# Scores computed transposed, softmax without the row maximum, row sums from a ones column beside V

## Chip, cores and metric

The kernel runs on one core of a Trainium2 chip. The metric is the device time of one execution in microseconds (us), from three executions; lower is better. TensorE (PE in the profile) does matrix products, VectorE (DVE), ScalarE (ACT) and GpSimd (POOL) do elementwise work, SyncE (SP) issues most transfers. PEld is TensorE's loading of weights, which the profile shows apart from the products.

## The reference

Input x has 128 graphs of 128 nodes with 768 features, adj is one 128x128 matrix a graph, about one entry in eight above zero. All is float32.

```python
h = jnp.maximum(_layernorm(x, axis=-1), 0.0)
q = _split_heads(h @ Wq + bq)            # 12 heads of 64
k = _split_heads(h @ Wk + bk)
v = _split_heads(h @ Wv + bv)
scores = jnp.einsum('bhqd,bhkd->bhqk', q, k) / jnp.sqrt(64)
scores = scores + beta * adj_e           # beta = 0.1
scores = jnp.where(adj_e > 0, scores, -9e15)
probs = jax.nn.softmax(scores, axis=-1)
out = jnp.einsum('bhqk,bhkd->bhqd', probs, v)
return x + out.transpose(0, 2, 1, 3).reshape(128, 128, 768)
```

## The kernel before

The 128 graphs go through in 32 groups G of four graphs g. Nodes lie on the 128 partitions. In a group the twelve heads go in six pairs; a pair is called oc, the same index as the 128 columns of Wq and Wk that belong to it, and j (0 or 1) is the head in the pair. So there are 32 x 6 = 192 pairs.

For each group, `norm` (lines 95 to 108) makes the normalised rows xn on VectorE with a power on GpSimd, and `to_hT` (110 to 116) transposes them on TensorE (tile pt) and takes them out of PSUM on ScalarE with the relu. `project_v` (118 to 127) makes V of the group with 96 matmul instructions of 384 columns. Every float32 matmul in the code is two matmul instructions in the trace; a transpose is one.

For each pair, `project_qk` (129 to 142) makes transposed Q and K of the four graphs, 12 instructions of 512 columns each (tiles pwq and pwk); VectorE takes Q out of PSUM, ScalarE takes K out. `scores` (144 to 165) makes 8 score blocks of 128x128 (tile sc; two heads on the upper and the lower 64 rows of the array). A row of a block is a query. Then, for each head of the pair and all four graphs at once, GpSimd fills a tile t with -9e15 (line 156), VectorE adds beta x adj (157), copies where adj is above zero (158) and reduces to the negative row maximum (160). ScalarE takes the exponential in 8 instructions a pair, one for each graph and head since the maximum is its bias, each with the row sum as a by-product that is read out by an instruction of its own (162). `transpose_probs` (167 to 176) transposes the 8 blocks on TensorE (tile ppt) and copies them out on ScalarE (pT), since the product with V needs keys on the partitions. `attend` (178 to 191) multiplies with V (tile av, 16 instructions of 64 columns), divides by the row sums on VectorE (187) and adds to x on GpSimd (189). When a group's last pair is added, SyncE sends its x out, and the x tile's next load waits for that.

The main loop (200 to 222) is a software pipeline over pairs: projections of pair i, transposes of pair i-1's probabilities, scores of pair i, product with V of pair i-1. Layer norm of the next group is placed in pairs 0 to 3 and its transposes in pairs 4 and 5. PSUM tiles of the tag mm (projections and pt) have three buffers, sc, pt two each, av one.

The order of instructions on each engine is not that of the code. A scheduler of the framework lays them out when the program is built, by its own estimates of times and by which buffers come free; each engine then runs its list strictly in that order and waits where an operand or a buffer is missing.

Of the kernel before, what the change touches and what calls it, by code (L numbers as in the profile page):

```python
# [9 lines left out]
F32 = mybir.dt.float32  # L10
U8 = mybir.dt.uint8
# [8 lines left out]
MASKED = -9000000000000000.0  # L20


@with_exitstack
def kernel(
# [26 lines left out]
    VH = D // 2  # L51
    SCALE = 1.0 / math.sqrt(HD)
# [8 lines left out]
    xs, bias, keep, xn, hT, vs = {}, {}, {}, {}, {}, {}  # L61
# [5 lines left out]
    def load_adj(G):  # L67
        a = big.tile([P, GRP, N], F32, tag="adj", name=f"adj_{G}")
        nc.sync.dma_start(a, adj[G * GRP:(G + 1) * GRP].rearrange("g q k -> q g k"))
        bias[G] = big.tile([P, GRP, N], F32, tag="bias", name=f"bias_{G}")  # L70
        nc.vector.tensor_scalar(bias[G], a, beta_c, None, op0=ALU.mult)
# [3 lines left out]
    load_x(0)  # L75
    ident = const.tile([P, P], F32, name="ident")
    make_identity(nc, ident)
    nhalf = const.tile([P, 1], F32, name="nhalf")
    nc.gpsimd.memset(nhalf, -0.5)
    beta_c = const.tile([P, 1], F32, name="beta_c")  # L80
# [29 lines left out]
    def to_hT(G, c):  # L110
        if c == 0:
            hT[G] = big.tile([P, NC, W], F32, tag="hT", name=f"hT_{G}")
        p = psum.tile([P, W], F32, tag="mm", name=f"pt_{G}_{c}", bufs=3)
        for g in range(GRP):
            nc.tensor.transpose(p[:, g * N:(g + 1) * N], xn[G][:, g, c * P:(c + 1) * P], ident)  # L115
        nc.scalar.activation(hT[G][:, c, :], p, AF.Relu)  # L116

    def project_v(G):
        vs[G] = big.tile([P, GRP, D], F32, tag="v", name=f"v_{G}")
        for g in range(GRP):  # L120
            for s in range(2):
                p = psum.tile([P, VH], F32, tag="mm", name=f"pv_{G}_{g}_{s}", bufs=3)
                for c in range(NC):
                    nc.tensor.matmul(p, hT[G][:, c, g * N:(g + 1) * N],  # L124
                                     w_sb["wv"][:, c, s * VH:(s + 1) * VH],
                                     start=(c == 0), stop=(c == NC - 1))
                nc.vector.tensor_add(vs[G][:, g, s * VH:(s + 1) * VH], p, bv_b[:, s * VH:(s + 1) * VH])  # L127

    def project_qk(G, oc):
        got = []  # L130
        for name in ("wq", "wk"):
            p = psum.tile([P, W], F32, tag="mm", name=f"p{name}_{G}_{oc}", bufs=3)
            for c in range(NC):
                nc.tensor.matmul(p, w_sb[name][:, c, oc * P:(oc + 1) * P], hT[G][:, c, :],  # L134
                                 start=(c == 0), stop=(c == NC - 1))
            t = work.tile([P, W], F32, tag=name, name=f"{name}T_{G}_{oc}", bufs=2)
            if name == "wq":
                nc.vector.tensor_scalar(t, p, bq_c[:, oc:oc + 1], SCALE, op0=ALU.add, op1=ALU.mult)  # L138
            else:
                nc.scalar.activation(t, p, AF.Identity, bias=bk_c[:, oc:oc + 1])  # L140
            got.append(t)
        return got

    def scores(G, oc, qT, kT):
        ps = [psum.tile([P, GRP, N], F32, tag="sc", name=f"sc_{G}_{oc}_{j}") for j in range(2)]
        for g in range(GRP):
            for j in range(2):
                r = slice(j * HD, (j + 1) * HD)
                nc.tensor.matmul(ps[j][:, g, :], qT[r, g * N:(g + 1) * N], kT[r, g * N:(g + 1) * N],  # L149
                                 start=True, stop=True)  # L150
        pr = []
        rs = stat.tile([P, 2, GRP], F32, tag="rs", name=f"rs_{G}_{oc}")
        sm = stat.tile([P, 2, GRP], F32, tag="sm", name=f"sm_{G}_{oc}")
        for j in range(2):
            t = work.tile([P, GRP, N], F32, tag="t", name=f"t_{G}_{oc}_{j}")
            nc.gpsimd.memset(t, MASKED)  # L156
            nc.vector.tensor_add(ps[j], ps[j], bias[G])  # L157
            nc.vector.copy_predicated(t, keep[G], ps[j])  # L158
            nmax = stat.tile([P, GRP], F32, tag="nmax", name=f"nmax_{G}_{oc}_{j}")
            nc.vector.tensor_reduce(nmax, t, AX.X, ALU.max, negate=True)  # L160
            for g in range(GRP):
                nc.scalar.activation(t[:, g, :], t[:, g, :], AF.Exp, bias=nmax[:, g:g + 1],  # L162
                                     accum_out=sm[:, j, g:g + 1])
            pr.append(t)
        return pr, sm, rs

    def transpose_probs(G, oc, pr):
        pT = []
        for j in range(2):
            p = psum.tile([P, GRP, N], F32, tag="pt", name=f"ppt_{G}_{oc}_{j}")  # L170
            for g in range(GRP):
                nc.tensor.transpose(p[:, g, :], pr[j][:, g, :], ident)  # L172
            t = work.tile([P, GRP, N], F32, tag="pT", name=f"pT_{G}_{oc}_{j}")
            nc.scalar.copy(t, p)  # L174
            pT.append(t)
        return pT

    def attend(G, oc, pT, sm, rs):
        nc.vector.reciprocal(rs, sm)
        pa = psum.tile([P, GRP, 2, HD], F32, tag="av", name=f"av_{G}_{oc}", bufs=1)  # L180
        for j in range(2):
            for g in range(GRP):
                h = 2 * oc + j
                nc.tensor.matmul(pa[:, g, j, :], pT[j][:, g, :], vs[G][:, g, h * HD:(h + 1) * HD],  # L184
                                 start=True, stop=True)
        o = work.tile([P, GRP, 2, HD], F32, tag="o", name=f"o_{G}_{oc}", bufs=2)
        nc.vector.tensor_mul(o, pa, rs.rearrange("p j g -> p g j")[:, :, :, None].to_broadcast([P, GRP, 2, HD]))  # L187
        xo = xs[G][:, :, oc * P:(oc + 1) * P]
        nc.gpsimd.tensor_add(xo, xo, o.rearrange("p g j d -> p g (j d)"))  # L189
# [3 lines left out]
    load_adj(0)  # L193
# [58 lines left out]
```

## Time and profile before

| what | value |
|---|---|
| median of three executions | 3869.4 us (3868.63 to 3870.0) |
| profiled execution: span from first to last instruction | 3866.2 us (its time beside the span is not given) |
| TensorE matmul busy, share of the span | 3825.9 us, 99% |
| TensorE weight loads busy | 2239.4 us, 58% |
| VectorE / ScalarE / GpSimd busy | 1402.0 / 1026.0 / 513.2 us (36%, 27%, 13%) |
| chain that ended last | PE 99%, DMA 1% |
| mean granted TensorE clock | 0.998 |

The chain of waits is followed back from the last instruction: at each step to what released it, or to the instruction before it on its engine. Its pieces add up to the span, so it tells what the time is made of, while busy times of one engine can overlap. A group row gives the busy time of all instructions of one line and shape, the mean duration of one, and the idle time before them with what ended it. Matmuls and weight loads are pipelined, so the mean duration of one is longer than its share of the busy time.

### The profile page before, as it was taken

Reading aid. Unit: us, or ns where it says so; the run is one execution under the profiler, and the core shown is the slowest. Engines: PE = TensorE matmul, PEld = TensorE weight load, DVE = VectorE, ACT = ScalarE, POOL = GpSimd, SP = SyncE. Lnnn points to the kernel's source line nnn. Section 1 sums busy time; section 2 is a strip of 40 time slices with the busy share of each in tenths; the row PEclk is TensorE's granted clock in tenths of the full one; section 3 lists DMA queues with packets and bytes.
Section 4 is the critical chain, followed back from the end, with each engine's and each line's share of the span. In section 5 each row is a group of like instructions: output and inputs, shape, how many; then the busy total and the mean of one; then the engine's idle time right before and its main releaser. Section 6 shows DMA issues by size and latency. Waiting matters only on the chain.

```text
span 3866.2 us, 41384 instructions
## 1 busy us (share of the span) xinstructions
PE 3825.9 (99%) x16128; PEld 2239.4 (58%) x16128; DVE 1402.0 (36%) x2688; ACT 1026.0 (27%) x3841; POOL 513.2 (13%) x711
## 2 busy tenths in 40 slices
PE   6999999999999999999999999999999999999998
PEld 3555555555555555555555555555555555555655
DVE  3343333333333433334333343333333333433323
ACT  1232222322222322223222232222332222322223
POOL 1011111111111111111111111111111111111111
PEclk9999999999999999999999999999999999999999
DMA  3000100100000100000010000000000000000000
GB/s 138 3 36 33 36 36 3 36 33 36 36 14 26 36 33 36 30 10 36 33 36 36 3 36 33 36 36 3 36 33 36 36 19 20 36 33 33 17 1 33
DMA packets 55330, 119.17 MB, mean 31 GB/s; under 512 B 3552, under 2 KB 19936, under 8 KB 55136
## 3 DMA queue, kind: packets, MB, share of 16 engines
q1 hardware_dynamic: 50688, 109.06, 7.7%
q10 hardware_dynamic: 4448, 7.48, 0.5%
q8 instruction: 127, 2.08, 0.2%
q14 instruction: 67, 0.55, 0.0%
HBM read 66.20 MB, written 50.33 MB: 30 GB/s over the span
## 4 chain that ended last, share of the span: by engine, by line
PE 99%; DMA 1%; issue 0%; DVE 0%; ACT 0%; POOL 0%; POOLq 0%
PE pwq L134 26%; PE pv L124 26%; PE pwk L134 26%; PE av L184 9%; PE sc L149 6%; PE ppt L172 4%; PE pt L115 2%; DMA x<-in_x_dram 0%; DMA adj<-in_adj_dram 0%; POOLq L247 0%; POOL x L189 0%; ACT L116 0%; DVE nmax L160 0%; DVE t L158 0%; DVE sc L157 0%
## 5 line engine op out<-in xcount | busy, mean ns | idle before, releaser
L134 PE MATMUL pwq<-hT,wq 128*128 128x512 f32 x2304 | 1032.5, 598 | 0.0
L134 PE MATMUL pwk<-hT,wk 128*128 128x512 f32 x2304 | 1020.1, 592 | 0.0
L124 PE MATMUL pv<-wv,hT 128*128 128x384 f32 x3072 | 996.0, 486 | 0.0
L124 PEld LDWEIGHTS pv<-wv,hT 128*128 128x128 f32 x3072 | 583.7, 190 | 413.9 <-issue 15.1
L134 PEld LDWEIGHTS pwk<-hT,wk 128*128 128x128 f32 x2304 | 437.8, 190 | 551.0 <-issue 543.4
L162 ACT ACTIVATE t<-t,nmax 128x128 f32<-128x128 f32 x1536 | 593.8, 392 | 486.4 <-DVE nmax L160 486.4
L134 PEld LDWEIGHTS pwq<-hT,wq 128*128 128x128 f32 x2304 | 422.9, 190 | 462.6 <-issue 452.5
L157 DVE TENSOR_TENSOR sc<-sc,bias 128x512 f32<-128x512 f32 x384 | 249.1, 694 | 979.6 <-PE sc L149 979.6
L127 DVE TENSOR_TENSOR v<-pv,bv_b 128x384 f32<-128x384 f32 x256 | 142.6, 557 | 1006.7 <-PE pv L124 1006.7
L156 POOL MEMSET t<- 128x512 f32 x384 | 189.2, 524 | 2262.9 <-PE ppt L172 2262.7
L174 ACT COPY pT<-ppt 128x512 f32<-128x512 f32 x384 | 204.5, 587 | 951.9 <-PE ppt L172 951.8
L140 ACT ACTIVATE wkT<-pwk,bk_c 128x512 f32<-128x512 f32 x192 | 131.9, 687 | 1193.0 <-PE pwk L134 1193.0
L184 PE MATMUL av<-v,pT 128*128 128x64 f32 x3072 | 385.4, 279 | 0.0
L189 POOL TENSOR_TENSOR x<-x,o 128x512 f32<-128x512 f32 x192 | 254.2, 1324 | 950.1 <-DVE o L187 950.1
L184 PEld LDWEIGHTS av<-v,pT 128*128 128x128 f32 x3072 | 359.0, 192 | 23.4 <-ACT pT L174 0.3
L162 ACT ACTIVATION_READ_ACCUMULATOR t<-t,nmax 128x1 f32 x1536 | 293.8, 191 | 0.0
L138 DVE TENSOR_SCALAR wqT<-pwq,bq_c 128x512 f32<-128x512 f32 x192 | 144.1, 751 | 355.9 <-PE pwq L134 353.5
L158 DVE COPY_PREDICATED t<-keep,sc 128x512 f32<-128x512 uint8 x384 | 255.7, 718 | 0.0
L160 DVE TENSOR_REDUCE nmax<-t 128x4 f32<-128x512 f32 x384 | 241.8, 670 | 0.0
L172 PEld LDWEIGHTS ppt<-ident,t 128*128 128x128 f32 x1536 | 180.2, 141 | 97.7 <-issue 90.0
L149 PE MATMUL sc<-wkT,wqT 64*128 64x128 f32 x3072 | 223.1, 285 | 0.0
L149 PEld LDWEIGHTS sc<-wkT,wqT 64*128 64x128 f32 x3072 | 186.3, 187 | 38.1 <-ACT wkT L140 32.3
(21 smaller groups left out, 1035.5 us busy)
## 6 DMA issues: line engine op xcount, KB each, us to landing
x<-in_x_dram SPq DMA_DIRECT2D x32, 1536.0 KB, 6.3
out_dram<-x SPq DMA_DIRECT2D x32, 1536.0 KB, 5.2
adj<-in_adj_dram SPq DMA_DIRECT2D x32, 256.0 KB, 2.5
wq<-in_L_gnn_Wq_dram ACTq DMA_DIRECT2D x6, 384.0 KB, 7.3
wk<-in_L_gnn_Wk_dram ACTq DMA_DIRECT2D x6, 384.0 KB, 9.1
wv<-in_L_gnn_Wv_dram ACTq DMA_DIRECT2D x6, 384.0 KB, 5.9
bv_b<-in_L_gnn_bv_dram ACTq DMA_DIRECT2D x1, 384.0 KB, 8.7
beta_c<-in_L_gnn_beta_dram ACTq DMA_DIRECT2D x1, 0.5 KB, 3.8
```

What stands on the lines that cost most here:

```text
L124: nc.tensor.matmul(p, hT[G][:, c, g * N:(g + 1) * N], w_sb["wv"][:, c, s * VH:(s + 1) * VH], start=(c == 0), stop=(c == NC - 1))
L134: nc.tensor.matmul(p, w_sb[name][:, c, oc * P:(oc + 1) * P], hT[G][:, c, :], start=(c == 0), stop=(c == NC - 1))
L149: nc.tensor.matmul(ps[j][:, g, :], qT[r, g * N:(g + 1) * N], kT[r, g * N:(g + 1) * N], start=True, stop=True)
L156: nc.gpsimd.memset(t, MASKED)
L157: nc.vector.tensor_add(ps[j], ps[j], bias[G])
L158: nc.vector.copy_predicated(t, keep[G], ps[j])
L160: nc.vector.tensor_reduce(nmax, t, AX.X, ALU.max, negate=True)
L162: nc.scalar.activation(t[:, g, :], t[:, g, :], AF.Exp, bias=nmax[:, g:g + 1], accum_out=sm[:, j, g:g + 1])
L172: nc.tensor.transpose(p[:, g, :], pr[j][:, g, :], ident)
L174: nc.scalar.copy(t, p)
L184: nc.tensor.matmul(pa[:, g, j, :], pT[j][:, g, :], vs[G][:, g, h * HD:(h + 1) * HD], start=True, stop=True)
L189: nc.gpsimd.tensor_add(xo, xo, o.rearrange("p g j d -> p g (j d)"))
```

## The change

The score product swaps its operands, so that a block comes out with keys on the partitions. The exponential of it can then go into the product with V as it is, and the transposes of the probabilities and their copies fall away. The row maximum, which would now lie across partitions, is not taken: VectorE does one instruction for each head (cap the score at 60, add the transposed bias), ScalarE one exponential of 128x512. Each head's V gets a 65th column of ones, which is filled once, so the product's 65th column is the row sum; it is raised to at least 1e-30, inverted and multiplied on VectorE. The product's tile av takes two PSUM banks, and mm gets four buffers in place of three.

The bias tile is new: `make_bias` makes beta x adj with -9e15 where adj is not above zero, transposes it on TensorE once a group (tile pb, four instructions), and ScalarE copies it out (biasT). It is called once ahead of the loop and then in pair 4 of each group but the last, for the next group.

Running maxima of the sums, of their inverses and of the squared bias are kept (`seen`, `seen_b`). After the last pair they are compared with caps (1e15, 1e15, 400), the result goes to a register of every engine, and a second program, `general`, runs behind a branch if a cap was passed. `general` is the same computation with the row maximum, one graph at a time, and writes all outputs anew.

The diff, cut to its core:

```diff
+SCORE_CAP = 60.0
+BIAS_CAP = 20.0
+SUM_CAP = 1e15
+TINY = 1e-30
...
+    bad = keep.tile([1, 1], I32, name="bad")
+    args = (x, adj, wq, bq, wk, bk, wv, bv, beta, out)
+    direct(tc, *args, bad)
+    again = nc.values_load(bad[0:1, 0:1])
+    with tc.If(again > 0):
+        general(tc, *args)
...
+    VE = HD + 1
...
-        a = big.tile([P, GRP, N], F32, tag="adj", name=f"adj_{G}")
-        nc.sync.dma_start(a, adj[G * GRP:(G + 1) * GRP].rearrange("g q k -> q g k"))
-        bias[G] = big.tile([P, GRP, N], F32, tag="bias", name=f"bias_{G}")
-        nc.vector.tensor_scalar(bias[G], a, beta_c, None, op0=ALU.mult)
-        keep[G] = big.tile([P, GRP, N], U8, tag="keep", name=f"keep_{G}")
-        nc.vector.tensor_scalar(keep[G], a, 0.0, None, op0=ALU.is_gt)
+        adjs[G] = big.tile([P, GRP, N], F32, tag="adj", name=f"adj_{G}", bufs=1)
+        nc.sync.dma_start(adjs[G], adj[G * GRP:(G + 1) * GRP].rearrange("g q k -> q g k"))
...
+    vs = [const.tile([P, GRP, HEADS, VE], F32, name=f"v{i}") for i in range(2)]
+    for v in vs:
+        nc.gpsimd.memset(v[:, :, :, HD:VE], 1.0)
...
-        p = psum.tile([P, W], F32, tag="mm", name=f"pt_{G}_{c}", bufs=3)
+        p = psum.tile([P, W], F32, tag="mm", name=f"pt_{G}_{c}", bufs=4)
...
+    def make_bias(G):
+        a = adjs[G]
+        b = work.tile([P, GRP, N], F32, tag="b", name=f"b_{G}", bufs=1)
+        nc.vector.tensor_scalar(b, a, beta_c, BIAS_CAP, op0=ALU.mult, op1=ALU.min)
+        kp = work.tile([P, GRP, N], U8, tag="kp", name=f"kp_{G}", bufs=1)
+        nc.vector.tensor_scalar(kp, a, 0.0, None, op0=ALU.is_gt)
+        bm = stat.tile([P, GRP], F32, tag="bm", name=f"bm_{G}", bufs=1)
+        b2 = work.tile([P, GRP, N], F32, tag="b2", name=f"b2_{G}", bufs=1)
+        nc.gpsimd.tensor_tensor(b2, b, b, ALU.mult)
+        nc.vector.tensor_reduce(bm, b2, AX.X, ALU.max)
+        nc.vector.tensor_tensor(seen_b, seen_b, bm, ALU.max)
+        nb = work.tile([P, GRP, N], F32, tag="nb", name=f"nb_{G}", bufs=1)
+        nc.gpsimd.memset(nb, MASKED)
+        nc.vector.copy_predicated(nb, kp, b)
+        p = psum.tile([P, GRP, N], F32, tag="mm", name=f"pb_{G}", bufs=4)
+        for g in range(GRP):
+            nc.tensor.transpose(p[:, g, :], nb[:, g, :], ident)
+        biasT[G] = big.tile([P, GRP, N], F32, tag="biasT", name=f"biasT_{G}")
+        nc.scalar.copy(biasT[G], p)
...
-                nc.vector.tensor_add(vs[G][:, g, s * VH:(s + 1) * VH], p, bv_b[:, s * VH:(s + 1) * VH])
+                nc.vector.tensor_add(v[:, g, s * HH:(s + 1) * HH, 0:HD],
+                                     p.rearrange("p (h d) -> p h d", d=HD),
+                                     bv_b[:, s * VH:(s + 1) * VH].rearrange("p (h d) -> p h d", d=HD))
...
-                nc.tensor.matmul(ps[j][:, g, :], qT[r, g * N:(g + 1) * N], kT[r, g * N:(g + 1) * N],
+                nc.tensor.matmul(ps[j][:, g, :], kT[r, g * N:(g + 1) * N], qT[r, g * N:(g + 1) * N],
                                  start=True, stop=True)
-        pr = []
-        rs = stat.tile([P, 2, GRP], F32, tag="rs", name=f"rs_{G}_{oc}")
-        sm = stat.tile([P, 2, GRP], F32, tag="sm", name=f"sm_{G}_{oc}")
+        es = []
         for j in range(2):
-            t = work.tile([P, GRP, N], F32, tag="t", name=f"t_{G}_{oc}_{j}")
-            nc.gpsimd.memset(t, MASKED)
-            nc.vector.tensor_add(ps[j], ps[j], bias[G])
-            nc.vector.copy_predicated(t, keep[G], ps[j])
-            nmax = stat.tile([P, GRP], F32, tag="nmax", name=f"nmax_{G}_{oc}_{j}")
-            nc.vector.tensor_reduce(nmax, t, AX.X, ALU.max, negate=True)
-            for g in range(GRP):
-                nc.scalar.activation(t[:, g, :], t[:, g, :], AF.Exp, bias=nmax[:, g:g + 1],
-                                     accum_out=sm[:, j, g:g + 1])
-            pr.append(t)
-        return pr, sm, rs
-
-    def transpose_probs(G, oc, pr):
-        pT = []
-        for j in range(2):
-            p = psum.tile([P, GRP, N], F32, tag="pt", name=f"ppt_{G}_{oc}_{j}")
-            for g in range(GRP):
-                nc.tensor.transpose(p[:, g, :], pr[j][:, g, :], ident)
-            t = work.tile([P, GRP, N], F32, tag="pT", name=f"pT_{G}_{oc}_{j}")
-            nc.scalar.copy(t, p)
-            pT.append(t)
-        return pT
-
-    def attend(G, oc, pT, sm, rs):
+            e = work.tile([P, GRP, N], F32, tag="e", name=f"e_{G}_{oc}_{j}")
+            nc.vector.scalar_tensor_tensor(e, ps[j], SCORE_CAP, biasT[G], op0=ALU.min, op1=ALU.add)
+            nc.scalar.activation(e, e, AF.Exp)
+            es.append(e)
+        return es
+
+    def attend(G, oc, es):
+        pa = psum.tile([P, 2, 512], F32, tag="av", name=f"av_{G}_{oc}", bufs=1)
+        for g in range(GRP):
+            for j in range(2):
+                at = ((g % 2) * 2 + j) * VE
+                nc.tensor.matmul(pa[:, g // 2, at:at + VE], es[j][:, g, :], vs[G % 2][:, g, 2 * oc + j, :],
+                                 start=True, stop=True)
+        got = pa[:, :, 0:4 * VE].rearrange("p a (b e) -> p a b e", e=VE)
+        sm = stat.tile([P, 2, 4, 1], F32, tag="sm", name=f"sm_{G}_{oc}")
+        nc.vector.tensor_scalar(sm, got[:, :, :, HD:VE], TINY, None, op0=ALU.max)
+        rs = stat.tile([P, 2, 4, 1], F32, tag="rs", name=f"rs_{G}_{oc}")
         nc.vector.reciprocal(rs, sm)
-        pa = psum.tile([P, GRP, 2, HD], F32, tag="av", name=f"av_{G}_{oc}", bufs=1)
-        for j in range(2):
-            for g in range(GRP):
-                h = 2 * oc + j
-                nc.tensor.matmul(pa[:, g, j, :], pT[j][:, g, :], vs[G][:, g, h * HD:(h + 1) * HD],
-                                 start=True, stop=True)
-        o = work.tile([P, GRP, 2, HD], F32, tag="o", name=f"o_{G}_{oc}", bufs=2)
-        nc.vector.tensor_mul(o, pa, rs.rearrange("p j g -> p g j")[:, :, :, None].to_broadcast([P, GRP, 2, HD]))
+        o = work.tile([P, 2, 4, HD], F32, tag="o", name=f"o_{G}_{oc}", bufs=2)
+        nc.vector.tensor_mul(o, got[:, :, :, 0:HD], rs.to_broadcast([P, 2, 4, HD]))
+        for i, t in enumerate((sm, rs)):
+            nc.vector.tensor_tensor(seen[:, i, :], seen[:, i, :], t.rearrange("p a b e -> p (a b e)"), ALU.max)
         xo = xs[G][:, :, oc * P:(oc + 1) * P]
-        nc.gpsimd.tensor_add(xo, xo, o.rearrange("p g j d -> p g (j d)"))
+        nc.gpsimd.tensor_add(xo, xo, o.rearrange("p a (b j) d -> p (a b) (j d)", j=2))
...
+    make_bias(0)
...
-                pT = transpose_probs(*prev[:3])
-            pr, sm, rs = scores(G, oc, qT, kT)
-            if prev is not None:
-                attend(*prev[:2], pT, *prev[3:])
-            prev = (G, oc, pr, sm, rs)
+                attend(*prev)
+            prev = (G, oc, scores(G, oc, qT, kT))
             if G + 1 < NG:
                 if oc < GRP:
                     norm(G + 1, oc)
...
                         to_hT(G + 1, c)
                 if oc == 1:
                     load_adj(G + 1)
+                if oc == 4:
+                    make_bias(G + 1)
...
-    attend(*prev[:2], transpose_probs(*prev[:3]), *prev[3:])
+    attend(*prev)
+
+    worst = stat.tile([P, 3], F32, tag="worst", name="worst")
+    nc.vector.tensor_reduce(worst[:, 0:2], seen, AX.X, ALU.max)
+    nc.vector.tensor_reduce(worst[:, 2:3], seen_b, AX.X, ALU.max)
+    over = stat.tile([P, 3], F32, tag="over", name="over")
+    nc.vector.tensor_scalar(over[:, 0:2], worst[:, 0:2], SUM_CAP, None, op0=ALU.is_gt)
+    nc.vector.tensor_scalar(over[:, 2:3], worst[:, 2:3], BIAS_CAP * BIAS_CAP, None, op0=ALU.is_ge)
+    pf = psum.tile([P, W], F32, tag="mm", name="pf", bufs=4)
+    nc.tensor.matmul(pf[0:1, 0:3], ones, over, start=True, stop=True)
+    nb_bad = stat.tile([1, 1], F32, tag="nbad", name="nbad")
+    nc.vector.tensor_reduce(nb_bad, pf[0:1, 0:3], AX.X, ALU.max)
+    nc.vector.tensor_copy(bad, nb_bad)
+
+
+@with_exitstack
+def general(ctx, tc, x, adj, wq, bq, wk, bk, wv, bv, beta, out):
```

The body of `general`, the constants beside it and the unchanged calls are left out.

Order on TensorE around pair 4 of a group before (G = 0; pwq and pwk are the projections, ppt the transposed probabilities, sc the scores, av the product with V, pt the next group's transposes; x4 and x6 are runs of the same row):

```order
L134 MATMUL pwq_4_589<-hT_157,wq 128x512 x6
L134 MATMUL pwk_4_598<-hT_157,wk 128x512 x6
L172 MATMUL ppt_3_0_607<-ident,t_3_0_546 128x128 x4
L172 MATMUL ppt_3_1_614<-ident,t_3_1_556 128x128 x4
L149 MATMUL sc_4_0_621<-wkT_4_605,wqT_4_596 128x128
L149 MATMUL sc_4_1_622<-wkT_4_605,wqT_4_596 128x128
...
L184 MATMUL av_3_654<-v_212,pT_3_0_612 128x64 x4
L184 MATMUL av_3_654<-v_212,pT_3_1_619 128x64 x4
L115 MATMUL pt_0_667<-ident,xn_309 128x128 x4
L115 MATMUL pt_1_673<-ident,xn_309 128x128 x4
L115 MATMUL pt_2_679<-ident,xn_309 128x128 x4
L134 MATMUL pwq_5_685<-hT_157,wq 128x512 x6
```

The same place on TensorE in the changed kernel (G = 1, where the layout has settled; e is the exponential, nb the masked bias, pb its transpose):

```order
L187 MATMUL pwq_4_1000<-hT_574,wq 128x512 x6
L187 MATMUL pwk_4_1009<-hT_574,wk 128x512 x6
L217 MATMUL av_3_1018<-v_121,e_3_0_984 128x65
L217 MATMUL av_3_1018<-v_121,e_3_1_987 128x65
...
L202 MATMUL sc_4_0_1036<-wqT_4_1007,wkT_4_1016 128x128
L202 MATMUL sc_4_1_1037<-wqT_4_1007,wkT_4_1016 128x128
...
L145 MATMUL pt_0_1053<-ident,xn_799 128x128 x4
L145 MATMUL pt_1_1059<-ident,xn_799 128x128 x4
L145 MATMUL pt_2_1065<-ident,xn_799 128x128 x4
L164 MATMUL pb_1083<-ident,nb_1080 128x128 x4
L187 MATMUL pwq_5_1090<-hT_574,wq 128x512 x6
```

The eight ppt rows are gone, the product with V of the pair before has moved ahead of the scores, and four pb rows stand behind pt and ahead of the next projection.

Order on VectorE behind the scores of pair 4 before (G = 0; t takes the masked scores, nmax the negative maximum, o is the divided product of the pair before):

```order
L157 TENSOR_TENSOR sc_4_0_621<-sc_4_0_621,bias_110 128x512
L157 TENSOR_TENSOR sc_4_1_622<-sc_4_1_622,bias_110 128x512
L158 COPY_PREDICATED t_4_0_633<-keep_112,sc_4_0_621 128x512
L158 COPY_PREDICATED t_4_1_643<-keep_112,sc_4_1_622 128x512
L160 TENSOR_REDUCE nmax_4_0_637<-t_4_0_633 128x4
L160 TENSOR_REDUCE nmax_4_1_647<-t_4_1_643 128x4
L187 TENSOR_TENSOR o_3_663<-av_3_654,rs_3_544 128x512
L179 RECIPROCAL rs_4_631<-sm_4_632 128x8
L138 TENSOR_SCALAR wqT_5_692<-pwq_5_685,bq_c 128x512
```

The same place on VectorE in the changed kernel (G = 0; b is beta x adj, kp the mask, bm the maximum of the squared bias, which GpSimd makes from b):

```order
L225 TENSOR_TENSOR o_3_553<-av_3_540,rs_3_551 128x512
L227 TENSOR_TENSOR seen<-seen,rs_3_551 128x8
L207 SCALAR_TENSOR_TENSOR e_4_0_568<-sc_4_0_558,biasT_221 128x512
L207 SCALAR_TENSOR_TENSOR e_4_1_571<-sc_4_1_559,biasT_221 128x512
L161 COPY_PREDICATED nb_1080<-kp_1073,b_1071 128x512
L151 TENSOR_SCALAR b_1549<-adj_1350,beta_c 128x512
L153 TENSOR_SCALAR kp_1551<-adj_1350 128x512
L157 TENSOR_REDUCE bm_1553<-b_3_1554 128x4
L158 TENSOR_TENSOR seen_b<-seen_b,bm_1553 128x4
L191 TENSOR_SCALAR wqT_5_619<-pwq_5_612,bq_c 128x512
```

The division o has moved ahead of the softmax rows of the next pair. The masked bias nb_1080 is written here, in group 0; the pb row that reads it is the one shown above on TensorE, in group 1. The scheduler has so moved the bias work a group ahead of the place where the code calls it, and b and kp, which stand behind the copy, are those of yet another group later.

More of the change, by code (lines that the diff above doesn't have):

```diff
@@ L10 @@
 F32 = mybir.dt.float32
+I32 = mybir.dt.int32
 U8 = mybir.dt.uint8
@@ L45, with direct @@
     nc = tc.nc
+    keep = ctx.enter_context(tc.tile_pool(name="keep", bufs=1))
+    bad = keep.tile([1, 1], I32, name="bad")
[5 more added lines that the diff above has]
+@with_exitstack
+def direct(ctx, tc, x, adj, wq, bq, wk, bk, wv, bv, beta, out, bad):
+    nc = tc.nc
     B, N, D = x.shape
@@ L59 @@
     psum = ctx.enter_context(tc.tile_pool(name="psum", bufs=2, space=bass.MemoryType.PSUM))
-    xs, bias, keep, xn, hT, vs = {}, {}, {}, {}, {}, {}
+    xs, adjs, biasT, xn, hT = {}, {}, {}, {}, {}
     def load_x(G):
@@ L79 @@
     nc.gpsimd.memset(nhalf, -0.5)
+    ones = const.tile([P, 1], F32, name="ones")
+    nc.gpsimd.memset(ones, 1.0)
+    seen = const.tile([P, 2, 2 * GRP], F32, name="seen")
+    nc.gpsimd.memset(seen, 0.0)
+    seen_b = const.tile([P, GRP], F32, name="seen_b")
+    nc.gpsimd.memset(seen_b, 0.0)
     beta_c = const.tile([P, 1], F32, name="beta_c")
@@ L116, in to_hT @@
         nc.scalar.activation(hT[G][:, c, :], p, AF.Relu)
+    def make_bias(G):
[17 more added lines that the diff above has]
+        nc.scalar.copy(biasT[G], p)
     def project_v(G):
-        vs[G] = big.tile([P, GRP, D], F32, tag="v", name=f"v_{G}")
+        v = vs[G % 2]
+        HH = HEADS // 2
         for g in range(GRP):
             for s in range(2):
-                p = psum.tile([P, VH], F32, tag="mm", name=f"pv_{G}_{g}_{s}", bufs=3)
+                p = psum.tile([P, VH], F32, tag="mm", name=f"pv_{G}_{g}_{s}", bufs=4)
                 for c in range(NC):
@@ new lines, in direct @@
+    nc.vector.tensor_scalar(over[:, 0:2], worst[:, 0:2], SUM_CAP, None, op0=ALU.is_gt)
[5 more added lines that the diff above has]
+    nc.vector.tensor_copy(bad, nb_bad)
+@with_exitstack
```

97 lines of the change are left out of this document (95 added, 2 removed).

## The prediction

> **What bounds the kernel now.** I read the page first: the span, the busy shares, and the chain that ended last.
>
> ```profile
> span 3866.2 us, 41384 instructions
> PE 3825.9 (99%) x16128; PEld 2239.4 (58%) x16128; DVE 1402.0 (36%) x2688; ACT 1026.0 (27%) x3841; POOL 513.2 (13%) x711
> PE pwq L134 26%; PE pv L124 26%; PE pwk L134 26%; PE av L184 9%; PE sc L149 6%; PE ppt L172 4%; PE pt L115 2%; DMA x<-in_x_dram 0%; DMA adj<-in_adj_dram 0%; POOLq L247 0%; POOL x L189 0%; ACT L116 0%; DVE nmax L160 0%; DVE t L158 0%; DVE sc L157 0%
> ```
>
> The whole chain is TensorE. What VectorE, ScalarE and GpSimd lose is worth nothing by itself; only TensorE's own list counts, and any wait in it. So the next view is the chain in order of time inside one group (start, length, what).
>
> ```profile
> 1029.55 0.87 PE ppt L172 x8
> 1030.42 1.09 PE sc L149 x16
> ...
> 1058.08 0.87 PE ppt L172 x8
> 1058.95 1.13 PE sc L149 x16
> 1060.08 1.93 PE av L184 x16
> 1062.01 5.21 PE pwq L134 x12
> 1067.21 5.15 PE pwk L134 x12
> ...
> 1090.58 1.32 PE pt L115 x12
> ```
>
> One pair takes 0.87 + 1.13 + 1.93 + 5.21 + 5.15 = 14.29 us. Over the whole span the projection of V shows the period of a group:
>
> ```profile
> 521.31 30.96 PE pv L124 x96
> 640.63 30.96 PE pv L124 x96
> ```
>
> 640.63 - 521.31 = 119.32 us, times 32 is 3818 us; start and tail are the other 48 us. The chain gives ppt 0.87 us a pair; that is the first term.
>
> **The change part by part.** *Transposes removed.* 192 pairs lose eight ppt instructions. The last pair's lie in the tail, counted below, so 191 x 0.87 = -166.2 us. Is the share of the chain the right price? Busy time is higher:
>
> ```profile
> L172 PE MATMUL ppt<-ident,t 128*128 128x128 f32 x1536 | 201.0, 273 | 2.1 <-ACT t L162 1.8
> L184 PE MATMUL av<-v,pT 128*128 128x64 f32 x3072 | 385.4, 279 | 0.0
> L184 PEld LDWEIGHTS av<-v,pT 128*128 128x128 f32 x3072 | 359.0, 192 | 23.4 <-ACT pT L174 0.3
> L149 PEld LDWEIGHTS sc<-wkT,wqT 64*128 64x128 f32 x3072 | 186.3, 187 | 38.1 <-ACT wkT L140 32.3
> ```
>
> 201.0 us counts the overlap with neighbours; it is the most that can go. I take the chain's 166 us, since it adds up to the period, and keep 201.0 for the range (35 us lower).
>
> *A small wait goes with them.* The last row says that the scores' weight loads stood 32.3 us behind ScalarE's copy of K. In the chain the scores take 1.13 us after a K projection, but 1.09 us where the long V projection lies between (1030.42). The product with V, 1.93 us long, now stands at that place, and K's copy has that time:
>
> ```profile
> L140 ACT ACTIVATE wkT<-pwk,bk_c 128x512 f32<-128x512 f32 x192 | 131.9, 687 | 1193.0 <-PE pwk L134 1193.0
> L174 ACT COPY pT<-ppt 128x512 f32<-128x512 f32 x384 | 204.5, 587 | 951.9 <-PE ppt L172 951.8
> L157 DVE TENSOR_TENSOR sc<-sc,bias 128x512 f32<-128x512 f32 x384 | 249.1, 694 | 979.6 <-PE sc L149 979.6
> ```
>
> 0.69 us fits under 1.93. Five pairs in six: 160 x 0.04 = -6.4 us.
>
> *Bias transposes added.* Four a group, priced as pt: 1.32 / 3 = 0.44 us. 31 groups: +13.6 us. The first group's are made at the start, where the chain has this:
>
> ```profile
> 33.56 2.82 PE pt L115 x12
> ```
>
> With three mm buffers, 12 of the 24 first transposes go ahead of the wait for ScalarE and these 12 behind it. With four buffers 16 go ahead, and 8 with the 4 new ones are left: 12 again, 0.
>
> *One column more.* Is the product with V set by its columns? Its loads are busy 359.0 / 3072 = 0.117 us each, its spacing is 1.93 / 16 = 0.121 us. The scores stream twice the columns at 1.13 / 16 = 0.071 us, with loads of half the rows, 186.3 / 3072 = 0.061 us. So the load sets it, not the columns, and the 65th is hidden: 0. Uncovered it costs 5.15 us / 12 / 512 = 0.84 ns, times 3072, 2.6 us. Swapped operands of the scores have the same shapes: 0.
>
> *Softmax, sums, maxima.* VectorE has for each head one instruction (as L157, 0.69 us) in place of three; ScalarE one of 128x512 (0.59 to 0.69 us by L174 and L140) in place of eight. Scores to exponentials for both heads: 2 x 0.69 + 0.69, about 2.1 us, and TensorE asks for them 10.36 us later, after pwq and pwk. Five small VectorE steps and four buffers instead of three change nothing there. Cover 8 us, price 0; without it, the 2.1 us a pair would cost 400 us.
>
> *The bias on VectorE and GpSimd.* In pair 4 the copy into nb waits for GpSimd's fill, which stands behind the addition to x. By the order, TensorE reads this nb only a group later, so it is never late: 0. Queued behind the copy are b, kp, the wait for GpSimd's square, then Q's copy of the next pair:
>
> ```profile
> L189 POOL TENSOR_TENSOR x<-x,o 128x512 f32<-128x512 f32 x192 | 254.2, 1324 | 950.1 <-DVE o L187 950.1
> L156 POOL MEMSET t<- 128x512 f32 x384 | 189.2, 524 | 2262.9 <-PE ppt L172 2262.7
> L158 DVE COPY_PREDICATED t<-keep,sc 128x512 f32<-128x512 uint8 x384 | 255.7, 718 | 0.0
> L71 DVE TENSOR_SCALAR bias<-adj,beta_c 128x512 f32<-128x512 f32 x32 | 15.2, 475 | 0.0
> L160 DVE TENSOR_REDUCE nmax<-t 128x4 f32<-128x512 f32 x384 | 241.8, 670 | 0.0
> ```
>
> From the end of the product with V: division about 1.2 us (0.69 below, and small steps), addition 1.32, fill 0.52, copy 0.72, b 0.48, square (as the addition) 1.32, reduction 0.67: 6.2 us. Q's copy has until the next scores, more than 10 us. Hidden with 4 us to spare.
>
> *x out and in.* The product with V of a group's last pair comes earlier, so its x goes out earlier, and the load behind it starts earlier:
>
> ```profile
> 1037.21 0.38 SPq L191 DMA_DIRECT2D out_dram<-x  x1
> 1042.40 0.37 SPq L65 DMA_DIRECT2D x<-in_x_dram  x1
> x<-in_x_dram SPq DMA_DIRECT2D x32, 1536.0 KB, 6.3
> L101 DVE BATCH_NORM_STATS2 st<-x 128x6 f32<-128x384 f32 x256 | 127.2, 530 | 15.5 <-DMA x<-in_x_dram 15.5
> ```
>
> Now the store starts 7.7 us after V's projection (1029.55); then about 1.93 + 1.2 + 1.32 + 0.2 = 4.7 us, so x lands at 4.7 + 5.2 + 6.3 = 16.2 us. VectorE asks for it in pair 1, ahead of that pair's softmax, at about 1.93 + 1.13 + 10.36 + 1.93 + 1.4 = 16.8 us. No wait, by 0.6 us. (The last row's 15.5 us lie at the start.)
>
> *Tail.* Now, from the timeline of the end:
>
> ```profile
> 3846.12 1.16 PE L149 MATMUL sc<-wkT,wqT 64*128 64x128 f32 x16
> ...
> 3847.22 2.00 PE L184 MATMUL av<-v,pT 128*128 128x64 f32 x16
> ...
> 3851.05 3.17 PE L172 MATMUL ppt<-ident,t 128*128 128x128 f32 x8 [1.84 <-ACT t L162]
> ...
> 3854.21 3.67 PE L184 MATMUL av<-v,pT 128*128 128x64 f32 x16
> 3857.98 0.69 DVE L187 TENSOR_TENSOR o<-av,rs 128x512 f32<-128x512 f32 x1 [4.05 <-PE av L184]
> 3860.04 0.37 SPq L191 DMA_DIRECT2D out_dram<-x  x1
> ```
>
> Scores to division are 3857.98 - 3846.12 = 11.9 us. Then: scores 1.16, two VectorE steps 1.3, exponential 0.6, product 3.67, small steps 0.4, handovers 0.3: 7.4 us, so 4.5 less. But the product of the last pair but one, which now runs beside the last softmax (3847.22), will stand ahead of the last scores: 1.93 more. So -2.6 us. The last product ran slow here, and the windows show why:
>
> ```profile
> 3847.00:3851.00 4.00, 2.21 (x22) 1.96 (x18) 3.68 (x7) 0.53 (x4) 0.00 (x0) 1.00 0.00 0
> 3854.00:3858.00 4.00, 3.89 (x17) 3.48 (x16) 0.02 (x1) 0.75 (x2) 0.00 (x0) 0.50 0.00 0
> ```
>
> The clock column (third from the end) fell to 0.50 after TensorE had stood 1.84 us and then, for 3.17 us, done eight transposes one by one. The changed tail has one gap of about 2 us. I keep 3.67 us; the bound is 1.93, a gain of 1.7 more. The Trainium skill, "TensorE: Matmul & The Clock Gate", section "What's actually happening", has the clock halved after an idle window of about 3.4 us; here the longest wait ahead of the fall was 1.84 us, with thin work behind it, so the trace neither bears out nor denies the length. By that rule the new gap would leave the clock whole, the sum 1.7 us lower.
>
> *Check and branch.* Two reductions, comparisons, one product, a register load and a branch come after the last sums. The last store runs 3866.2 - 3860.04 = 6.2 us beside them, and before it the division and addition, so I take 0. No row shows a branch taken far ahead; bounds are 0 and, if it started only behind the store, another 6 us or so, the length of the nearest row, a store. Against the change stands the Trainium skill, "Runtime: NRT & Kernel Launch", section "Instruction fetch mechanics": a taken branch out of the fetched window waits for a fetch of its target; no run here shows one, and it states no time for it, so the sum by it lies inside the same bounds.
>
> *Sum.* -166.2 - 6.4 + 13.6 - 2.6 = -161.6 us. Span 3866.2 - 161.6 = 3704.6 us. The median is 3.2 us above the profiled span, taken as what lies around it: 3708 us. Bounds: 35 us lower by busy time; above, 2.6 (column), 6 (branch), and 192 x 0.06 = 11.5 if the new neighbours cost what pwq shows over pwk (5.21 against 5.15).
>
> **The rivals.** *The bias comes too late.* If nb were written in the pair that reads it, TensorE, at 1.13 + 1.32 = 2.45 us after the product with V, would wait for division, addition, fill and copy, 3.8 us: 1.4 us in 30 groups, 42 us, so 3750. The order, with nb a group ahead, speaks against it. 7 in 100.
>
> *The 65-column rows stream badly.* Rows 260 bytes apart could cost a second pass. That shows only if loads and columns add up: 64 x 0.84 ns x 3072 = 165 us, so 3873, no change. The scores' 0.071 us at 128 columns speaks against it. 3 in 100.
>
> *VectorE stands behind x, slower than before.* The statistics of the loaded x stand in VectorE's list ahead of pair 1's softmax, with 0.6 us of margin. Behind the first lie the softmax steps (1.4 us), seven more (0.53 each) and small ones, some 6.5 us up to Q's copy at about 24 us; the scores that need it come at 28.8, which leaves about 5 us before TensorE notices. Then each microsecond costs one in 29 groups. Slower than before means 161.6 / 29 = 5.6 us of wait, x about 11 us later than worked out. Landing took 6.3 us as the median, so it would have to take 17; for it speaks only the thin margin. At 14 us of lateness: 29 x 8.4 = +244 us, 3952. 3 in 100.
>
> *The branch is taken.* Then `general` does all products again, the projections alone three times 26% of the span, 3,000 us: over 6,700. From the reference's inputs the row sums lie between 2.2 and 87.7 and beta x adj below 0.1, against caps of 1e15 and 20. 2 in 100.
>
> **How the numbers follow.** Forecast 85 in 100, 3708 us. Its own bounds are 3708 - 35 - 1.7 = 3671 and 3708 + 20 = 3728; the lower end needs all overlap to go, so I cut it to 3684. To hold part of the late bias, which could come in part, I go up to 3740. The measurement tells apart about 0.2%, 7.7 us. Faster: forecast and late bias, 92 in 100. Same: 3. Slower: 5.
>
> **What would show it.** In the changed profile: no ppt; the chain of a pair with av 1.93, sc 1.09, pwq and pwk 10.36, so 13.38 us; group period 119.32 - 6 x 0.87 - 5 x 0.04 + 0.44 = 114.34 us; pb with no TensorE wait on nb; x statistics with no wait on a transfer. An av row above 2 us, waits of pb on VectorE or of sc on Q, or a period above 116 us would make the prediction wrong.

## The result and the profile after

The changed kernel takes 3696.45 us (median of four, 3694.58 to 3698.57) against 3869.7 us before (median of four too; the 3869.4 us ahead is of three). The ratio is 0.9553, 95% interval 0.9539 to 0.9566: 4.5% faster. The forecast was 3708 us, with a range of 3684 to 3740. Of the profiled execution the span is 3692.5 us and the time 3694.58 us, so 2.1 us lie around the span, where 3.2 us had been taken from the median.

First the page of the changed kernel: the span, the busy shares, and the chain by line.

```profile
span 3692.5 us, 34646 instructions
PE 3648.3 (99%) x14722; PEld 2100.4 (57%) x14722; DVE 1036.9 (28%) x2598; ACT 474.3 (13%) x801; POOL 367.7 (10%) x396
PE pwq L187 27%; PE pv L175 27%; PE pwk L187 27%; PE av L217 9%; PE sc L202 6%; PE pt L145 3%; PE pb L164 0%; DMA adj<-in_adj_dram 0%; DMA x<-in_x_dram 0%; DVE xn L138 0%; POOL rstd L137 0%; DVE st L131 0%; DVE o L225 0%; ACT L146 0%; ACT e L208 0%
```

TensorE is as full as before, with the ppt line gone. ScalarE lost over half of its busy time and VectorE a quarter, and both have 0% of the chain. Next the chain in order of time: one ordinary pair, then pair 4 with the next group's transposes pt and the bias transposes pb.

```profile
1015.39 1.73 PE av L217 x16
1017.12 1.09 PE sc L202 x16
1018.21 5.35 PE pwq L187 x12
1023.56 5.15 PE pwk L187 x12
...
1042.03 1.73 PE av L217 x16
1043.76 1.09 PE sc L202 x16
1044.86 1.46 PE pt L145 x12
1046.32 0.44 PE pb L164 x4
1046.75 5.15 PE pwq L187 x12
```

A pair takes 13.32 us (13.38 forecast). But two pieces differ from the forecast: the product with V is down from 1.93 to 1.73, and what stands behind the scores is up, pwq from 5.21 to 5.35 and pt from 1.32 to 1.46. The V projections give the period of a group:

```profile
502.38 30.96 PE pv L175 x96
616.24 30.96 PE pv L175 x96
```

113.85 us (616.24 - 502.38, to the rounding), where 114.34 was forecast and 119.32 was before. Among the waits, neither pb on its bias nor the scores on Q or K show up on TensorE. VectorE's wait for x is this row (sum, times, longest):

```profile
DVE st L131 <- DMA x<-in_x_dram: 13.1, 7, 8.9
```

8.9 of the 13.1 us are the start. The other six waits sum to 4.2 us in 30 groups: the thin margin was gone in these, and nothing on TensorE followed.

### The profile page after: what moved, and what is told of

Read it like the earlier page. It is cut to its first block, busy times and chain, and to the rows that moved or that the text cites. A ratio compares the mean times of both kernels' runs of the same rounds, so it can differ in the third digit from the quotient of the medians.

```text
span 3692.5 us, 34646 instructions
## 1 busy us (share of the span) xinstructions
PE 3648.3 (99%) x14722; PEld 2100.4 (57%) x14722; DVE 1036.9 (28%) x2598; ACT 474.3 (13%) x801; POOL 367.7 (10%) x396
## 3 DMA queue, kind: packets, MB, share of 16 engines
q8 instruction: 118, 1.93, 0.2%
## 4 chain that ended last, share of the span: by engine, by line
PE 99%; DMA 1%; DVE 0%; ACT 0%; POOL 0%; issue 0%; ACTq 0%; DVEq 0%; POOLq 0%
PE pwq L187 27%; PE pv L175 27%; PE pwk L187 27%; PE av L217 9%; PE sc L202 6%; PE pt L145 3%; PE pb L164 0%; DMA adj<-in_adj_dram 0%; DMA x<-in_x_dram 0%; DVE xn L138 0%; POOL rstd L137 0%; DVE st L131 0%; DVE o L225 0%; ACT L146 0%; ACT e L208 0%
## 5 line engine op out<-in xcount | busy, mean ns | idle before, releaser
L217 PEld LDWEIGHTS av<-v,e 128*128 128x128 f32 x3072 | 373.2, 192 | 86.8 <-issue 76.5
L208 ACT ACTIVATE e<-e 128x512 f32<-128x512 f32 x384 | 231.2, 627 | 1382.5 <-DVE e L207 1381.6
L217 PE MATMUL av<-v,e 128*128 128x65 f32 x3072 | 364.2, 272 | 1.7 <-ACT e L208 1.7
L207 DVE SCALAR_TENSOR_TENSOR e<-sc,biasT 128x512 f32<-128x512 f32 x384 | 246.3, 683 | 0.8 <-PE sc L202 0.6
L202 PE MATMUL sc<-wqT,wkT 64*128 64x128 f32 x3072 | 223.1, 285 | 0.0
L202 PEld LDWEIGHTS sc<-wqT,wkT 64*128 64x128 f32 x3072 | 186.3, 187 | 13.5 <-issue 0.5
L131 DVE BATCH_NORM_STATS2 st<-x 128x6 f32<-128x384 f32 x256 | 132.0, 534 | 13.4 <-DMA x<-in_x_dram 13.1
L225 DVE TENSOR_TENSOR o<-av,rs 128x512 f32<-128x512 f32 x192 | 132.8, 692 | 9.4
L145 PE MATMUL pt<-ident,xn 128*128 128x128 f32 x768 | 101.2, 282 | 30.9 <-DVE xn L138 15.7
L146 ACT ACTIVATE hT<-pt 128x512 f32<-128x512 f32 x192 | 106.9, 595 | 165.2 <-PE pt L145 165.0
```

Of the source, the lines that this page charges most:

```text
L131: nc.vector.bn_stats(st[:, s, :], xg[:, s * VH:(s + 1) * VH])
L202: nc.tensor.matmul(ps[j][:, g, :], kT[r, g * N:(g + 1) * N], qT[r, g * N:(g + 1) * N], start=True, stop=True)
L207: nc.vector.scalar_tensor_tensor(e, ps[j], SCORE_CAP, biasT[G], op0=ALU.min, op1=ALU.add)
L208: nc.scalar.activation(e, e, AF.Exp)
L217: nc.tensor.matmul(pa[:, g // 2, at:at + VE], es[j][:, g, :], vs[G % 2][:, g, 2 * oc + j, :], start=True, stop=True)
L225: nc.vector.tensor_mul(o, got[:, :, :, 0:HD], rs.to_broadcast([P, 2, 4, HD]))
```

## Experiments

Theory A is the prediction's: only TensorE's own list counts, so the gain is the transposes that left it. Its rival S: the lighter softmax on VectorE and ScalarE carries part of the gain. For the two pieces that had not been foreseen there are theory P, that whatever stands behind the scores pays, and rival Q, that the new order of heads made the product itself faster.

**The old softmax without the transposes.** Edit of the kernel before, with `transpose_probs` left uncalled:

```diff
-                pT = transpose_probs(*prev[:3])
-            pr, sm, rs = scores(G, oc, qT, kT)
-            if prev is not None:
-                attend(*prev[:2], pT, *prev[3:])
+                attend(*prev)
+            pr, sm, rs = scores(G, oc, qT, kT)
```

> The kernel before, with its whole softmax (maximum, mask copy, eight exponentials with sums), without the eight transposes of the probabilities and their copies, and with the product with V ahead of the scores; the product so takes the probabilities untransposed, which changes what is computed. Theory A, only TensorE's list counts: the group falls to the changed kernel's 113.85 us less its 0.44 us of bias transposes, 113.4 us, the time to about 3681 us (3672 to 3690), below the changed kernel. Rival S, the lighter softmax on VectorE and ScalarE carries part of the gain: with the old softmax the time stays well above the changed kernel's 3696 us, about 3780 if it carries half.

Measured 3685.7 us, ratio to before 0.9522 (0.9506 to 0.9538). Busy shares and chain of this kernel:

```profile
PE 3640.3 (99%) x14592; PEld 2089.5 (57%) x14592; DVE 1397.9 (38%) x2688; ACT 846.1 (23%) x3457; POOL 515.7 (14%) x711
...
1014.52 1.73 PE av L184 x16
1016.25 1.09 PE sc L149 x16
1017.34 5.35 PE pwq L134 x12
1022.69 5.15 PE pwk L134 x12
...
1045.44 5.23 PE pwq L134 x12
```

VectorE and GpSimd are as busy as before. ScalarE has 846 us against 1026; the pT copies, 204.5 us before, are gone. Still the pair is the changed kernel's, piece by piece. S falls: the old softmax costs the end nothing. The kernel is even faster than the changed one, by 10.8 us. It makes no bias transposes (0.44 us a group) and has no check; against that, the last line, the projection behind pt, is 5.23 us as before and not 5.15. This kernel has three mm buffers.

**The light softmax with the transposes.** Edit of the changed kernel, beside putting `transpose_probs` back ahead of the scores (its tiles now take mm's four buffers, and nb gets two):

```diff
-                nc.tensor.matmul(ps[j][:, g, :], kT[r, ...], qT[r, ...],
+                nc.tensor.matmul(ps[j][:, g, :], qT[r, ...], kT[r, ...],
...
-        for g in range(GRP):
-            nc.tensor.transpose(p[:, g, :], nb[:, g, :], ident)
-        nc.scalar.copy(biasT[G], p)
+        biasT[G] = nb
```

> The changed kernel with the score operands swapped back, the transposes of the probabilities and their copies put back, the bias not transposed; the light softmax, the ones column, the check and the branch stay. Theory A: the pair goes back to 14.29 us, the time to about 3870 us (3860 to 3880). Rival S: it stays below 3800 us, since the softmax is light. On the product with V, which stands behind the scores again but keeps the new order of heads and 65 columns: if whatever follows the scores pays (theory P), its share of the chain is 1.93 us; if the new order or tile layout made the product itself faster (rival Q), 1.73 us, and the time is about 3832 us.

Measured 3859.5 us, ratio 0.9972 (0.9961 to 0.9982). Its chain:

```profile
1044.19 0.87 PE ppt L213 x8
1045.07 1.09 PE sc L198 x16
1046.16 1.93 PE av L224 x16
1048.09 5.21 PE pwq L183 x12
...
1090.84 1.31 PE pt L145 x12
1092.15 5.15 PE pwq L183 x12
```

The product is back at 1.93 us and the projection at 5.21, though the product has the new order of heads and 65 columns. That is P and against Q. S falls here too: with the light softmax, and the transposes kept, almost nothing is gained. 10.7 us of gain are left, and the time lies just under the expected 3860 to 3880. From its V projections, which start at 166.10 and 3735.59 us with 30 periods between, the period is 118.98 us, 0.34 less than before. The pieces are 5 x 0.04 for the scores (1.09, not 1.13) and 2 x 0.08 for the projection behind pt (5.15, not 5.23).

**Heads in the old order.** Edit of the changed kernel:

```diff
-        for g in range(GRP):
-            for j in range(2):
+        for j in range(2):
+            for g in range(GRP):
```

> The changed kernel with the product with V in the old order, all four graphs of one head and then of the other. Theory P: the product stays at 1.73 us and the next projection at 5.35, the time at 3696 us (3693 to 3700). Rival Q: the alternation of the heads made the product faster, so it goes back towards 1.93 us a pair, the time to as much as 3734 us.

Measured 3696.06 us (3694.35 to 3696.2). In its chain the product is 1.73 and the projection behind the scores 5.35. Q falls.

**The product partly behind the scores.** Edit of the changed kernel:

```diff
-                attend(*prev)
-            prev = (G, oc, scores(G, oc, qT, kT))
+            es = scores(G, oc, qT, kT)
+                attend(*prev)
+            prev = (G, oc, es)
```

> The changed kernel with the product with V called behind the scores. The scheduler still pulls 14 of its 16 instructions ahead of the scores, as ScalarE's copy of K is due only then; the last two come behind them. Theory P, whatever follows the scores pays once: the two take 0.22 + 0.20 = 0.42 us, the projection behind them goes from 5.35 to 5.21, what the kernel before shows behind a product, so a pair gains 0.06 us of length and the time is 8 to 12 us more, about 3706 us. Rival: the 5.35 belongs to the projection itself in the new kernel (another operand layout, VectorE reading beside it): it stays, and the two take 0.22 us; the time stays at 3696 us.

Measured 3702.9 us (3701.69 to 3705.53). Its chain:

```profile
1017.81 1.51 PE av L217 x14
1019.31 1.09 PE sc L202 x16
1020.41 0.36 PE av L217 x2
1020.77 5.20 PE pwq L187 x12
...
1047.41 1.31 PE pt L145 x12
1048.73 0.44 PE pb L164 x4
1049.16 5.29 PE pwq L187 x12
```

The payment moves with the position: two instructions of the product, 0.22 us at the pace of the others (1.51 / 14 each), take 0.36, while pwq and pt fall back to 5.20 and 1.31. The pair is 13.32 us again, not 0.06 longer as expected; the two paid 0.14, not 0.20. The time is 6.4 us more than the changed kernel's, where 8 to 12 were expected, and the period 0.19 us longer. That comes from two other places. In pair 4 the projection behind pb takes 5.29 us and not 5.15: its first weight load starts 0.05 us behind ScalarE's copy of the first pt tile, which now stands behind an exponential. In pair 0, where the scheduler left the whole product behind the scores, the pieces come to 0.06 us more.

Where the payment arises can be read from the weight loads. Before and after alike, the load behind the scores starts 0.12 us after the last score load has ended (191 of 192 pairs), while a projection's load behind the product starts 0.08 us before the load ahead of it has ended. Why a load comes so late behind the scores is not shown.

**Sixty-four columns.** Edit of the changed kernel, the column before the ones now stands for the sum:

```diff
-                nc.tensor.matmul(pa[:, g // 2, at:at + VE], es[j][:, g, :], vs[G % 2][:, g, 2 * oc + j, :],
+                nc.tensor.matmul(pa[:, g // 2, at:at + HD], es[j][:, g, :], vs[G % 2][:, g, 2 * oc + j, 0:HD],
...
-        nc.vector.tensor_scalar(sm, got[:, :, :, HD:VE], TINY, None, op0=ALU.max)
+        nc.vector.tensor_scalar(sm, got[:, :, :, HD - 1:HD], TINY, None, op0=ALU.max)
```

> The changed kernel with a product of 64 columns, without the ones column; the 64th column of V's product stands in for the row sums, so the division is by something else. If the weight load sets the product's pace, as the prediction had it: the product stays at 1.73 us a pair, the time at 3696 us. If columns count: 1.72 us, 2.6 us less in all; if rows of 65 with 260 bytes between them stream at half pace: far less than 1.73 us, up to 160 us less in all.

Measured 10516.9 us. A column of the product can be negative, unlike a sum; raised to 1e-30 its inverse passes the cap, and the branch was taken. So this run prices the second program: 10516.9 - 3696.5 = 6820 us more, in part at half the granted clock (mean 0.894 over the run, 0.998 in the changed kernel). The first program, up to 3688 us, still answers the question. From its timeline:

```profile
960.90 31.12 PE L175 MATMUL pv<-wv,hT 128*128 128x384 f32 x96
991.86 1.89 PE L217 MATMUL av<-v,e 128*128 128x64 f32 x16
...
1074.75 31.12 PE L175 MATMUL pv<-wv,hT 128*128 128x384 f32 x96
```

The period is 1074.75 - 960.90 = 113.85 us, the changed kernel's to the hundredth. The 65th column costs nothing.

**Three mm buffers.** Edit of the changed kernel: every `tag="mm"` tile has `bufs=3` in place of 4.

> The changed kernel with three mm buffers in place of four. The prediction had the fourth buffer at nothing but the first transposes: then 3696 us, up to 1 us more at the start. The rival: in pair 4 the projection behind the bias transposes would take the buffer of the second pt tile, which ScalarE empties only behind both exponentials, about 1 us after TensorE is ready for it in the changed kernel's timeline; then TensorE waits 1 to 1.5 us in each of 31 groups, 3727 to 3743 us, unless the scheduler lays ScalarE's list out anew.

Measured 3711.2 us (3710.76 to 3711.95), 14.7 us more than with four: neither of the two numbers. Its chain in pair 4:

```profile
1049.71 0.60 PE pt L145 x4
...
1050.34 0.60 ACT hT L146
1050.93 1.04 ACT e L208 x2
...
1052.02 1.11 PE av L217 x8
1053.13 5.20 PE pwq L187 x12
```

The chain leaves TensorE for ScalarE here. By the timeline the three pt tiles run through and fill all three buffers, and the bias transposes behind them start 0.05 us after ScalarE's copy of the first tile has ended. The scheduler laid the list out anew: ten instructions of the next product are brought forward ahead of the projection, and their weight loads wait 0.10 us for the first exponential and 0.22 us for the second. The period is (3591.84 - 162.31) / 30 = 114.32 us by the starts of its V projections, 0.47 us over the changed kernel's. The exponentials do reach TensorE where a buffer is short.

**Without check and branch.** Edit of the changed kernel: the code from `worst` to `bad`, `values_load` and `general` are left out; `seen` is still kept.

> The changed kernel without the final check, the register load, the branch and the second program; the running maxima are still kept. If the check and branch lie wholly beside the last store, as the prediction had it: no change, 3696 us. If they do not, as the 9.2 us from the last store's issue to the end of the span (6.2 before) suggest: 3 us less, 3693 us, and 6.2 us from that issue to the end.

Measured 3692.0 us (3691.67 to 3694.4) against 3696.45: the spans, 3689.9 and 3692.5, differ by 2.6 us. The last store of each, first of the changed kernel:

```profile
3683.31 0.37 SPq L231 DMA_DIRECT2D out_dram<-x  x1
```

and of the kernel without the branch:

```profile
3683.53 0.37 SPq L228 DMA_DIRECT2D out_dram<-x  x1
```

From there to the end of the span it is 9.2 us with and 6.4 us without. Check and branch are not hidden beside the store; they cost 2.8 us.

**Weights issued by SyncE.** Edit of the changed kernel:

```diff
-            nc.scalar.dma_start(w_sb[name][:, c, :], src[c * P:(c + 1) * P, :])
+            nc.sync.dma_start(w_sb[name][:, c, :], src[c * P:(c + 1) * P, :])
```

> The changed kernel with the 18 weight transfers issued by SyncE behind x and adj of the first group, not by ScalarE. In the changed kernel ScalarE is done with issuing at 33.4 us and only then copies the first transposes, and the first projection starts at 38.2 us. If ScalarE's issuing is what holds the start: the first projection at about 22 us, when the last layer norm (19 us) is transposed, and the time 16 us less, 3680 us. If the transfers themselves hold it: first projection still above 33 us, 3692 to 3696 us.

Measured 3680.2 us (3679.3 to 3680.58), ratio to before 0.9509 (0.9494 to 0.9525): 16.3 us less than the changed kernel, the fastest version here. The start of the chain, first in the changed kernel and then here:

```profile
33.46 1.28 ACT L146
34.75 0.61 ACT hT L146
...
38.23 5.33 PE pwq L187 x12
```

```profile
19.57 0.61 ACT hT L146
...
23.05 5.39 PE pwq L187 x12
```

ScalarE's issuing, not the transfers, held the first projection.

## Why the prediction was right, and where it was off

The forecast was right in sign, in cause and within the range, 11.6 us too high. The span fell by 3866.2 - 3692.5 = 173.7 us, forecast 161.6. By its steps:

- *Transposes removed, -166.2 us.* Right, mechanism and price. They are wholly on TensorE's list: the old softmax without them gains all of it, the new softmax with them almost none.
- *The wait for K's copy, -6.4 us.* Right. Before, the first score load starts 0.05 us after K's copy has ended, in 159 of 192 pairs; in the changed kernel the copy has ended at least 0.87 us ahead of it, under the product, as forecast. With the transposes kept the scores take 1.09 us too, but for another reason: there K's copy starts 0.04 us after the last K product and not 0.10 us, so the load no longer waits for it (it comes 0.17 us after the transposes' last load, and 0.20 us where it waited). Why the copy starts earlier stays open.
- *Bias transposes, +0.44 us a group.* Measured 0.44, with no wait on nb. The order with nb a group ahead held, and the rival of the late bias did not come.
- *Swapped neighbours, taken as 0 with up to 11.5 us above.* This step failed in its bounds, which were on one side only: a gain had been left out. Leaving the scores costs what follows 0.14 to 0.20 us, before and after. Before, the product paid it, and the projection behind the product another 0.06. Now pwq or pt pays, and the product has the long projection ahead of it. Per group: the product 6 x -0.20, pwq 4 x +0.14, pt 2 x +0.14, together -0.36 us, 11.2 us in 31 groups.
- *Four buffers change nothing.* Wrong. The projection behind pt went from 5.23 to 5.15 us, 2 x 0.08 us a group or 5 us in all. Before, pt's three tiles hold all three buffers, and the projection's first weight load starts 0.05 us after ScalarE's copy of the first tile has ended (62 of 63 times):

```profile
1091.06 1.57 ACT L116 ACTIVATE hT<-pt 128x512 f32<-128x512 f32 x3 [2.67 <-PE pt L115]
1091.71 0.30 PEld L134 LDWEIGHTS pwq<-hT,wq 128*128 128x128 f32 x2
```

In the changed kernel it follows the transposes without a gap:

```profile
1046.48 0.30 PEld L187 LDWEIGHTS pwq<-hT,wq 128*128 128x128 f32 x2
```

With three buffers the changed kernel takes 14.7 us more.
- *One column more, 0.* Right.
- *Softmax and sums, cover of 8 us.* Right with four buffers; with three, a part of it is on the path.
- *Start, 0.* It was 1.9 us later (first projection at 38.23, before 36.38), as ScalarE was done with issuing its transfers later. Why the transfers took that much longer was not tried.
- *Tail, -2.6 us with the product at the slow clock.* The product ran at full clock, by luck:

```profile
3678.28 0.44 PE L217 MATMUL av<-v,e 128*128 128x65 f32 x2 [1.54 <-ACT e L208]
3678.88 1.82 PE L217 MATMUL av<-v,e 128*128 128x65 f32 x14 [0.16 <-ACT e L208]
```

1.82 us for 14 instructions behind a wait of 1.54 us, so 1.8 us better than forecast. The windows show the granted clock (third from the end):

```profile
3676.00:3681.00 5.00, 3.01 (x30) 2.49 (x26) 2.32 (x8) 1.23 (x2) 1.27 (x1) 0.95 0.00 0
3681.00:3684.00 3.00, 0.19 (x2) 0.09 (x2) 2.46 (x8) 0.00 (x0) 1.26 (x1) 0.50 0.00 0
```

It fell to 0.50 at about 3680.5 us, as the last instructions of this product ran. In the 64-column run the last product also waits 1.54 us, but there the clock fell at 3681.7 us, just behind the product's start at 3681.45, and its last 14 instructions take 3.25 us:

```profile
3682.05 3.25 PE L217 MATMUL av<-v,e 128*128 128x64 f32 x14
```

The Trainium skill, "TensorE: Matmul & The Clock Gate", section "What's actually happening", has the clock halved after an idle window of about 3.4 us; by that rule this gap would leave it whole. The traces do not agree: in both runs the clock fell, and the longest wait of TensorE just ahead of it was 1.54 us.
- *Check and branch, 0, bounds 0 and 6.* Measured 2.8 us. Which part the branch has in it, and which the register load and the joining at the end, stays open. Instructions are fetched there: from 3680 to 3693 us the two instruction queues of the changed kernel move five packets, all from about 3688.4 us on, behind the check. The kernel without the branch moves none behind its last store.

```profile
q8 instruction: 2, 0.03, 0.9%
q14 instruction: 3, 0.02, 0.4%
```

The Trainium skill, "Runtime: NRT & Kernel Launch", section "Instruction fetch mechanics", has a taken branch out of the fetched window wait for a fetch of its target. The packets agree with a fetch; how long anything waited for it no run shows.

Sum of the differences: -11.2 - 5.0 + 1.9 - 1.8 + 2.8 = -13.3 us, against -12.1 measured; most of the rest is the rounding of the pieces: by the periods, 114.34 and 113.85 us, 31 groups gave 15.2 us, not 16.2.

Of the rivals, slow 65-column rows are ruled out by the 64-column run. x did come late in six groups, by 4.2 us in all, without reaching TensorE. The branch was not taken; taken, it costs 6820 us, where the rival had put some 3,000.

## What to carry to other kernels

Where one engine's list is the whole chain, count what leaves that list and what enters it; work saved on the engines beside it was worth nothing here, though it is most of what the change removes. Price the neighbours of a removed step too, with bounds on both sides: here a change of what follows what was worth 11 us, and a buffer count that looked free decided whether the covered engines stay covered. A fallback behind a branch costs little while it is not taken (2.8 us here), but its trigger must be tested against what the sums can be.

## What was not expected of the hardware

- Whatever TensorE runs right behind the score products, which use 64 rows of the array each, takes 0.14 to 0.20 us more than elsewhere, and the cost moves with the position (product 1.93 or 1.73, pwq 5.35 or 5.15 to 5.21, pt 1.46 or 1.31). That the 64 rows are the reason was not tested.
- The granted clock fell to 0.50 behind a wait of TensorE of 1.54 us with full work on both sides, at 3680.5 us in the changed kernel and at 3681.7 us in the 64-column run; whether the last product ran at 1.82 or 3.25 us for 14 instructions hung on that moment.
- ScalarE, with 18 weight transfers on its queue, did no other work until 33.4 us; on SyncE's queue the same transfers left the first projection free at 23.05 us.
